# The order of instructions of a four-layer graph kernel, searched again with a store that counts until it lands

## The chip, the cores and the metric

The kernel runs on one core of one Trainium2 chip. The metric is the device time of one execution in microseconds (us), the median over several runs. A separate execution is recorded by the hardware profiler; its span can differ from the timed runs by a few microseconds. The engines are PE (matmul), DVE (vector), ACT (activation), POOL (GpSimd) and SP (SyncE, which here only issues transfers). PEld is PE's loading of weights, which runs beside its matmuls.

## The reference, cut to what matters

128 graphs of 64 nodes with 256 features go through four layers. Each layer is followed by a residual addition and a layer norm.

```python
# layer 0: gated graph network, five rounds l
m = h @ weight[l];  agg = A^T @ m           # A = (adj != 0)
h = gru_cell(agg, h)                        # r, z, n gates; tanh and sigmoid
x = layernorm(x + h * mask)
# layer 1: graph network with a wide hidden layer
h = (epsilon * x + adj @ x) @ W1 + b1       # 256 -> 1024
x = layernorm(x + silu(rmsnorm(h) * rms_weight) @ W2 + b2)
# layer 2: hyperbolic layer
x = layernorm(x + project(expmap0(adj @ logmap0(x))))
# layer 3: attention over neighbours
h = x @ W_w.T + W_b;  u = adj * exp(e_i + f_j + a_b)
x = layernorm(x + (u / sum(u)) @ h)
```

## The kernel before

Two graphs stand side by side on the 128 partitions, with a block-diagonal adjacency; four such blocks, eight graphs, form a group. There are 16 groups, and each passes through all four layers on its own. One extra stream ahead of them prepares weights. All is in 32-bit floats. The large products of layer 0 and of the first half of layer 1 use seven products of half blocks instead of eight (`gate`, `prod` and the sums in `sums`, lines 733 to 761), which costs DVE additions.

Memory is held in three sets of slots (`NF = 3`): group g uses set g % 3. A tile's tag says which slot it takes, and most tags have one buffer. Tag A holds, in one group, the tile `tA` of each round of layer 0 (L736, the differences of the state's halves), then the outputs of norms, and at the very end `o`, the result of the last `layer_norm`, from which the store to `out` is issued (L1116). Three groups later the same slot takes `tA` again, so the first subtraction of that group waits until the store has read the slot.

No instruction is placed by hand. `group(g)` records operations with a price in us for each engine that could do them, and with the buffers they read and write. `Flow.issue` then replays a planner, `Plan.advance`, which picks from up to four open groups (`WINDOW`) the operation that could start first by the plan's clocks, prices, waits for other operations (`HOPS` between engines), free PSUM banks (eight) and outstanding transfers. Ties and priorities are given by a rank: 0 prefers the oldest group, 1 the youngest (loads apart), and 2 and up the groups' remaining path minus a lag from `LAGS` per group. The string `CHOICES` has one digit for each stretch of planned time (`STRETCH`) and says which rank holds in it. The string was found by a search outside the kernel; the kernel only replays it. The resulting order is forced on each engine. Semaphores are placed by the framework from the data dependencies.

A transfer's operation has a size `kb`. Then the plan adds to its end a start cost, the transfer over a common bus and a landing cost, `DMA = (2.0, 330.0, 1.0)`, and whatever depends on it is ready only then:

```python
if o.kb:
    self.bus = max(self.bus, end + flow.DMA[0]) + o.kb / flow.DMA[1]
    end = self.bus + flow.DMA[2]
```

The final store carries no `kb`, so in the plan its slot is free 0.1 us after it starts. Some operations are marked `port`: those of POOL and a number of DVE operations with two inputs in SBUF. The plan lets no two of these overlap. The comparisons of adjacency blocks (L706), their rewriting (L896) and the small operations of the norms (L678, L1018 to L1041) carry no such mark.

The norms of all but the last two groups take the mean from sums gathered earlier, squares on ACT (L665), a power on POOL (L676) and a scaling on ACT or DVE (`scaled`, L334 and L335); the last two groups use DVE's statistics instead (L672).

Of the kernel before, what the change touches and what calls it, by code (L numbers as in the profile page):

```python
# [13 lines left out]
AF = mybir.ActivationFunctionType  # L14
OP = mybir.AluOpType
# [11 lines left out]
class Buf:  # L27


    def __init__(self, make, slot=None, bank=False):  # L30
        self.make, self.slot, self.bank = make, slot, bank
        self.ap, self.uses, self.left, self.after = None, [], 0, ()
# [21 lines left out]
class Plan:  # L54


    def __init__(self, flow):
        self.flow = flow
        ops = [o for s in flow.streams for o in s]
        self.need = [o.need for o in ops]  # L60
        self.at = [0.0] * len(ops)
        self.uses = {}
        self.clock = dict.fromkeys(flow.AHEAD, 0.75)
        self.queues = [{e: deque(o for o in s if e in o.ways) for e in self.clock} for s in flow.streams]
        self.banks = [0.0] * BANKS
        self.left, self.first, self.bus = len(ops), 0, 0.0
        self.lands = [0.0] * flow.TRANSFERS
        self.order, self.table, self.port = [], None, 0.0
# [60 lines left out]
class Flow:  # L129
# [11 lines left out]
    AHEAD = {"PE": 32, "DVE": 10, "ACT": 10, "POOL": 4, "SP": 2}  # L141


    HOPS = {"from PE": 0.25, "to PE": 0.3, "else": 0.1, "own": 0.0}

    SOONER = 0.4

# [2 lines left out]
    TRANSFERS = 8  # L150

    TABLE = 1.28
    WINDOW, STRETCH, LAGS = 4, 7.0, (0.0, 60.0, 150.0)
    CHOICES = ("0120330330303130310011121010201001100010002001222000010013000330100101111033330000333001101130100330"
               "0000031033000310101000311310101010000013101101101100010000013103010010101000100330110330000113003003"
               "1300130130100000010113001030300100100110333311103310110001000111110011110100111010130010011313010301"
               "110003301001110311310110011010200100000")

    BEHIND = mybir.DependencyInfo(mybir.DependencyClass.NoSync, mybir.DependencyReason.DATA)

# [44 lines left out]
    def hop(self, e, to):  # L205
        if e == to:
            return 0.0 if e == "PE" else self.HOPS["own"]
        return self.HOPS["from PE" if e == "PE" else "to PE" if to == "PE" else "else"]

# [11 lines left out]
    def issue(self):  # L221
        self.ways()
        ranks = (lambda s, o: (s, o.n), lambda s, o: (s if o.kb else -s, o.n), *(lambda s, o, lag=lag: (lag * s - o.way, s, o.n) for lag in self.LAGS))
        plan, until = Plan(self), 0.0
        for c in self.CHOICES:
            until += self.STRETCH
# [12 lines left out]
def kernel(  # L239
# [31 lines left out]
    nc = tc.nc  # L271
# [19 lines left out]
    flow = Flow(tc)  # L291
# [6 lines left out]
    def bank(name):  # L298
        return Buf(lambda: psum.tile([P, 512], F32, tag="bank", name=name), bank=True)
# [11 lines left out]
        return nc.tensor.matmul(o, lhsT, rhs, start=(k == 0), stop=(k == nk - 1))  # L311

    def pe(n, run, w, r):
        flow.op("PE", {512: 0.86, 256: 0.435, 128: 0.23, 1: 0.21}.get(n, 0.3), run, w, r)

    def turn(run, w, r):
        flow.op("PE", 0.11, run, w, r)
# [1 line left out]
    def dve(n, run, w, r, port=False):  # L319
        flow.op("DVE", 0.145 + 0.00105 * n, run, w, r, port=port)  # L320
# [3 lines left out]
    def act(n, run, w, r, sets=None):  # L324
        flow.op("ACT", 0.22 + 0.00077 * n, run, w, r, sets=sets)
# [5 lines left out]

    def scaled(n, o, i, scale, bias, w, r, port=()):

        flow.either([("ACT", 0.22 + 0.00077 * n, lambda: nc.scalar.activation(o(), i(), AF.Identity, bias=bias(), scale=scale())),  # L334
                     ("DVE", 0.145 + 0.00105 * n, lambda: nc.vector.tensor_scalar(o(), i(), scale(), bias(), OP.mult, OP.add))], w, r, port=port)  # L335

    def pool(us, run, w, r=()):
        flow.op("POOL", us, run, w, r, port=True)
# [5 lines left out]
    out_rows = out.rearrange("(g b t) n d -> g (t n) b d", b=NB, t=2)  # L344
# [45 lines left out]
    pow2 = const.tile([P, 2, NB], F32, name="pow2")  # L390
# [121 lines left out]
    for l in range(L):  # L512
        ps = bank("ps_wmT")
# [8 lines left out]
        for k in range(KD):  # L522
            for i, n in ((0, 2 * D), (1, D)):
                ps = bank("ps_wmih")
# [71 lines left out]
    def group(g):  # L596
        s = g % NF

        def tiny(name, shape=(P, NB), dt=F32):
            t = f"{name}{s}"  # L600
            return Buf(lambda: small.tile(list(shape), dt, tag=t, name=f"{name}_{g}"), slot=(t, 2))
# [54 lines left out]
        def layer_norm(y, st, tag, name, norm=None):  # L656

            mv = tiny("mv", (P, NB, 2))
            ve, rstd, off = tiny("ve", (P, 2, NB)), tiny("rstd", (P, 2, NB)), tiny("off")
            o = rows(tag, f"x_{name}")  # L660
            m = 2 if norm else 1
            if summed:
                dve(4, lambda: nc.vector.tensor_scalar(mv[:, :, 0], st[:, :, 0], -1.0 / D, None, OP.mult), [mv], [st])
                for b in range(NB):
                    act(500, lambda b=b: nc.scalar.activation(  # L665
                        o[:, b, :], y[:, b, :], AF.Square, bias=mv[:, b, 0:1], accum_out=st[:, b, 1:2]),
                        [(o, b), (st, (1, b))], [(y, b), mv])
                dve(8, lambda: nc.vector.scalar_tensor_tensor(  # L668
                    ve[:, :m, :], over(st[:, :, 1], m), 1.0 / D, eps2[:, :m, :], OP.mult, OP.add), [ve], [st])
            else:  # L670
                for b in range(NB):
                    dve(256, lambda b=b: nc.vector.bn_stats(st[:, b, :], y[:, b, :]), [(st, b)], [(y, b)])  # L672
                    dve(4, lambda b=b: nc.vector.bn_aggr(mv[:, b, :], st[:, b, :]), [(mv, b)], [(st, b)])
                dve(8, lambda: nc.vector.tensor_tensor(
                    ve[:, :m, :], over(mv[:, :, 1], m), eps2[:, :m, :], OP.add), [ve], [mv])
            pool(1.1, lambda: nc.gpsimd.tensor_tensor(rstd[:, :m, :], ve[:, :m, :], pow2[:, :m, :], OP.pow), [rstd], [ve])  # L676
            if norm:
                dve(4, lambda: nc.vector.scalar_tensor_tensor(  # L678
                    norm.tile(), rstd[:, 1, :], float(np.sqrt(D)), rstd[:, 0, :], OP.mult, OP.mult), [norm], [rstd])
            dve(4, lambda: nc.vector.scalar_tensor_tensor(  # L680
                off.tile(), mv[:, :, 0], 1.0 if summed else -1.0, rstd[:, 0, :], OP.mult, OP.mult), [off], [mv, rstd])
            for b in range(NB):
                scaled(256, lambda b=b: o[:, b, :], lambda b=b: y[:, b, :], lambda b=b: rstd[:, 0, b:b + 1],
                       lambda b=b: off[:, b:b + 1], [(o, b)], [(y, b), off, rstd], ("DVE",))
            return o
# [3 lines left out]
        if g == NG - 2:  # L689


            for k in range(KD):
                w = unit("h", (NG - 3) % NF, f"w1_{k}", (P, H), 2)
# [4 lines left out]
        ps = bank("ps_adjT")  # L698
# [189 lines left out]
        for n in range(2):  # L888
            ps = rows_of(hT, n)
            for j in range(2):  # L890
                b = 2 * n + j
# [93 lines left out]
        ps = bank("ps_ss")  # L985
# [16 lines left out]
        for h in range(NB // 2):  # L1002
            ps = bank("ps_o1")
            for j in range(2):
                b = 2 * h + j
# [6 lines left out]
        xn = tiny("n")  # L1012
        x2 = layer_norm(y1, st1, "A", "n1", xn)


        rn, fac, n2, ser = (tiny(t) for t in ("rn", "fac", "n2", "ser"))
        near = tiny("near", dt=I32)
# [11 lines left out]
        def series():  # L1029
# [5 lines left out]
                  for q in (11, 9, 7, 5, 3)),  # L1035
                v.tensor_add(ser.tile(), ser.tile(), one4),
                v.scalar_tensor_tensor(near.tile(), xn.tile(), SERIES_BELOW, one4, OP.is_lt, OP.mult)]
        dve(1150, series, [n2, ser, near], [xn])
        dve(4, lambda: nc.vector.scalar_tensor_tensor(fac.tile(), fac.tile(), 0.5, rn.tile(), OP.mult, OP.mult),
            [fac], [fac, rn])  # L1040
        dve(4, lambda: nc.vector.copy_predicated(fac.tile(), near.tile(), ser.tile()), [fac], [fac, near, ser])  # L1041
        tan = rows("B", "tan")
        for b in range(NB):
            flow.either([
                ("DVE", 0.3, lambda b=b: nc.vector.tensor_scalar(tan[:, b, :], x2[:, b, :], fac[:, b:b + 1], None, OP.mult)),
                ("ACT", 0.37, lambda b=b: nc.scalar.activation(tan[:, b, :], x2[:, b, :], AF.Identity, scale=fac[:, b:b + 1]))],
                [(tan, b)], [(x2, b), fac])
        us = tiny("ss")
        y2 = rows("y", "y2")
# [1 line left out]
        for h in range(NB // 2):  # L1051
            for j in range(2):
                b = 2 * h + j
                pe(256, lambda b=b, j=j, ps=sup[h]: matmul(
                    ps[:, j * D:(j + 1) * D], adjT[:, b, :], tan[:, b, :], 0, 1), [sup[h]], [adjT, (tan, b)])
            for j in range(2):
                b = 2 * h + j
# [32 lines left out]
        for b in range(NB):  # L1090
            ps = bank("ps_a")
            for k in range(KD):
                pe(256, lambda ps=ps, b=b, k=k: matmul(
                    ps[:, :D + 2], x3T[:, k, b * P:(b + 1) * P], wattT[:, k, :], k, KD), [ps], [(x3T, b // 2), wattT])
            act(4, lambda ps=ps, b=b: nc.scalar.activation(
                hw[:, b, D:], ps[:, D:D + 2], AF.Exp, bias=cs.tile()), [(hw, b)], [ps, cs], EXP)
            flow.either([
                ("ACT", 0.37, lambda ps=ps, b=b: nc.scalar.activation(
                    hw[:, b, :D], ps[:, :D], AF.Identity, scale=hw[:, b, D:D + 1])),
                ("DVE", 0.37, lambda ps=ps, b=b: nc.vector.tensor_scalar(  # L1100
                    hw[:, b, :D], ps[:, :D], hw[:, b, D:D + 1], None, OP.mult))], [(hw, b)], [ps, (hw, b)])
# [6 lines left out]
        for b in range(NB):  # L1108
            ps = bank("ps_att")
# [3 lines left out]
            dve(4, lambda b=b: nc.vector.tensor_mul(rd[:, b:b + 1], rd[:, b:b + 1], hw[:, b, D + 1:]), [(rd, b)], [(rd, b), (hw, b)])  # L1113
            onto_rows(y3, b, st3, ps, 0, lambda b=b: rd[:, b:b + 1], x3, [(rd, b)])
        o = layer_norm(y3, st3, "A", "n3")
        flow.op("SP", 0.1, lambda: nc.sync.dma_start(out_rows[g], o.tile()), (), [o])  # L1116

    for g in range(NG):
        flow.stream()
# [34 lines left out]
```

## Time and profile before

| | |
|---|---|
| time, median of 3 runs | 2393.74 us (2393.57 to 2394.22) |
| span in the profile | 2397.7 us |
| PE busy | 2338.0 us, 98% |
| PE's weight loads busy | 2045.3 us, 85% |
| DVE, ACT, POOL busy | 1878.5, 1248.8, 343.4 us |
| last PE instruction ends before the span's end | 11.8 us |
| output stores | 16 of 512 KB, median 2.9 us from issue to landing |

A matmul record's end is modelled, so the sum of single durations means little here; the idle time of PE and the share of the clock that it was granted say how far the span is from PE's own work. Numbers in the timeline count from the first instruction. A line number is that of the kernel; many products share the lines of helpers, so tiles tell them apart.

### The profile page before, as it was taken

The numbers are of one execution on the slowest core, as the hardware profiler recorded it, in microseconds if no ns is written. First come the engines' busy times: TensorE is split into PE (matmuls) and PEld (weight loads), VectorE is DVE, ScalarE is ACT, GpSimd is POOL, SyncE is SP. The second block draws the span as 40 slices with busy tenths as digits, with TensorE's granted clock in tenths as the row PEclk, the third lists the DMA queues.
The fourth block names the chain that finished last, engine by engine and source line by source line (L and its number), as shares of the span: only waits on it lengthen the run. The fifth ranks groups of instructions, "written<-read, shape, count | busy, mean of one in ns | idle before, by whom it ended". The sixth has DMA issues, their size and how long they took to land.

```text
span 2397.7 us, 32662 instructions
## 1 busy us (share of the span) xinstructions
PE 2338.0 (98%) x11938; PEld 2045.3 (85%) x11938; DVE 1878.5 (78%) x4291; ACT 1248.8 (52%) x2671; POOL 343.4 (14%) x272
## 2 busy tenths in 40 slices
PE   9999998999999999999999999999999999999986
PEld 8888887888888888888888888888888888888854
DVE  6778978778878878778778788868877886887866
ACT  3333455666455555465555555554454467445364
POOL 1300111411010201112120110210111131011011
PEclk9999999999999999999999999999999999999998
DMA  3000001000000000000000000000000000000000
GB/s 122 10 1 1 12 1 38 1 21 1 29 1 27 3 1 30 1 27 3 1 29 1 29 1 27 3 7 23 1 10 21 10 1 21 27 1 10 27 9 18
DMA packets 39728, 36.22 MB, mean 15 GB/s; under 512 B 9956, under 2 KB 38656, under 8 KB 39568
## 3 DMA queue, kind: packets, MB, share of 16 engines
q1 hardware_dynamic: 37840, 32.25, 4.3%
q8 instruction: 95, 1.56, 0.3%
q10 hardware_dynamic: 1328, 1.31, 0.2%
q0 software_dynamic: 400, 0.57, 0.1%
q14 instruction: 65, 0.53, 0.1%
HBM read 25.74 MB, written 8.39 MB: 14 GB/s over the span
## 4 chain that ended last, share of the span: by engine, by line
PE 91%; DVE 5%; ACT 2%; DMA 1%; issue 1%; POOL 0%; ACTq 0%; POOLq 0%; DVEq 0%
PE p_v L753 11%; PE p_w L753 11%; PE p_r L753 11%; PE ps_o L311 9%; PE ps_agg L311 7%; PE p_hy L759 6%; PE p_u L753 6%; PE p_iy L759 6%; PE p_ix L759 4%; PE p_hx L759 4%; PE ps_hr L627 3%; PE ps_a L311 2%; PE p_vh L940 2%; PE p_1h L940 2%; PE p_wh L940 2%; PE ps_wmih L311 1%
## 5 line engine op out<-in xcount | busy, mean ns | idle before, releaser
L676 POOL TENSOR_TENSOR rstd<-ve,pow 128x4 f32<-128x4 f32 (+1 forms) x64 | 79.5, 1242 | 1296.9 <-DVE ve L668 1186.5
L311 PE MATMUL ps_o<-w2s,hid 128*128 128x256 f32 x1024 | 234.2, 381 | 0.3 <-ACT hid L1000 0.3
L311 PEld LDWEIGHTS ps_o<-w2s,hid 128*128 128x128 f32 x1024 | 194.3, 191 | 26.5 <-ACT hid L1000 0.3
L753 PE MATMUL p_v<-tA,w_h 128*128 128x256 f32 x640 | 172.7, 380 | 0.8 <-DVE V L804 0.8
L753 PE MATMUL p_v<-tB,w_a 128*128 128x256 f32 x640 | 171.4, 379 | 0.0
L753 PE MATMUL p_r<-hT,w_h 128*128 128x256 f32 x640 | 171.1, 382 | 0.2 <-ACT U L329 0.2
L753 PE MATMUL p_r<-agg,w_a 128*128 128x256 f32 x640 | 167.1, 381 | 0.2 <-ACT agg L329 0.2
L807 ACT ACTIVATE U<-U,half_b 128x512 f32<-128x512 f32 (+1 forms) x160 | 93.9, 628 | 133.6 <-DVE U L804 133.4
L311 PEld LDWEIGHTS ps_agg<-edge,hr 128*128 128x128 f32 x1024 | 138.3, 191 | 7.9 <-ACT hr L329 0.2
L329 ACT COPY agg<-ps_agg 128x512 f32<-128x512 f32 x148 | 86.1, 583 | 109.6 <-PE ps_agg L311 108.4
L311 PE MATMUL ps_agg<-edge,hr 128*128 128x128 f32 x1024 | 140.3, 275 | 0.0
L759 PE MATMUL p_hy<-tA,w_hn 128*128 128x256 f32 x480 | 131.9, 381 | 6.9 <-DVE tA L736 4.7
L329 ACT COPY hr<-ps_hr 128x512 f32<-128x512 f32 x120 | 70.1, 584 | 129.2 <-PE ps_hr L627 128.5
L779 DVE SCALAR_TENSOR_TENSOR hnb<-p_hy,half_b,hs 128x256 f32<-128x256 f32 x240 | 108.6, 479 | 35.3 <-PE p_hy L759 34.0
L753 PEld LDWEIGHTS p_r<-agg,w_a 128*128 128x128 f32 x640 | 120.4, 191 | 16.5 <-ACT agg L329 0.9
L759 PE MATMUL p_iy<-tB,w_in 128*128 128x256 f32 x480 | 132.3, 383 | 2.2 <-DVE V L824 2.2
L753 PEld LDWEIGHTS p_v<-tA,w_h 128*128 128x128 f32 x640 | 119.2, 191 | 16.7 <-DVE V L804 1.2
L753 PEld LDWEIGHTS p_v<-tB,w_a 128*128 128x128 f32 x640 | 119.7, 190 | 16.0 <-issue 0.5
L807 ACT ACTIVATE V<-V,half_b 128x256 f32<-128x256 f32 (+1 forms) x160 | 87.2, 585 | 80.5 <-DVE V L804 80.2
L753 PEld LDWEIGHTS p_r<-hT,w_h 128*128 128x128 f32 x640 | 116.0, 191 | 13.8 <-ACT U L329 0.4
L1000 ACT ACTIVATE hid<-hid,cols 128x512 f32<-128x512 f32 x128 | 85.5, 717 | 62.9 <-DVE hid L998 62.8
L334 ACT ACTIVATE x_n<-y,off,rstd 128x256 f32<-128x256 f32 x173 | 90.8, 589 | 45.4 <-DVE off L680 45.4
(262 smaller groups left out, 5819.4 us busy)
## 6 DMA issues: line engine op xcount, KB each, us to landing
x<-in_x_dram SPq DMA_DIRECT2D x16, 512.0 KB, 3.6
xr<-in_x_dram SPq DMA_DIRECT2D x16, 512.0 KB, 3.4
out_dram<-x_n SPq DMA_DIRECT2D x16, 512.0 KB, 2.9
edge<-in_adj_dram SPq DMA_DIRECT2D x32, 64.0 KB, 2.3
wm<-in_L_gnn_weight_dram SPq DMA_DIRECT2D x5, 256.0 KB, 5.1
w2s<-in_L_gnn_W_dram SPq DMA_DIRECT2D x1, 1024.0 KB, 9.0
w<-in_L_gnn_W_dram SPq DMA_DIRECT2D x2, 512.0 KB, 3.4
w_in_L_gnn_w_hh_dram<-in_L_gnn_w_hh_dram ACTq DMA_DIRECT2D x1, 512.0 KB, 5.4
```

What stands on the lines that cost most here:

```text
L311: return nc.tensor.matmul(o, lhsT, rhs, start=(k == 0), stop=(k == nk - 1))
L329: flow.either([("ACT", 0.22 + 0.00077 * n, lambda: nc.scalar.copy(o(), i())), ("DVE", 0.145 + 0.00105 * n, lambda: nc.vector.tensor_copy(o ...
L334: flow.either([("ACT", 0.22 + 0.00077 * n, lambda: nc.scalar.activation(o(), i(), AF.Identity, bias=bias(), scale=scale())), ("DVE", 0.145 ...
L627: turn(lambda j=j, c=c: nc.tensor.transpose(ps[:, j * D + c * P:j * D + (c + 1) * P], src[:, c, (2 * n + j) * P:(2 * n + j + 1) * P], iden ...
L676: pool(1.1, lambda: nc.gpsimd.tensor_tensor(rstd[:, :m, :], ve[:, :m, :], pow2[:, :m, :], OP.pow), [rstd], [ve])
L753: pe(256, lambda i=i, w=w, c=c: nc.tensor.matmul(ps[:, c * HR:(c + 1) * HR], w[:, m, c * P:(c + 1) * P], v[i][0](), start=first and i == 1 ...
L759: pe(256, lambda: nc.tensor.matmul(ps[:, j * HR:(j + 1) * HR], w[:, m, :], v[0](), start=first, stop=True, skip_group_check=True), [ps], [ ...
L779: dve(300, lambda: nc.vector.scalar_tensor_tensor(out(n, c)(), ps[:, j * HR:(j + 1) * HR], b(c), x(), OP.add, OP.add), [(hnb, (n, c))], [p ...
L807: act(256 if len(w) == 1 else 512, lambda: nc.scalar.activation(o(), src(), AF.Tanh, bias=half_b[:, i * KD + c:i * KD + c + 1], scale=0.5) ...
L940: pe(256, lambda c=c: nc.tensor.matmul(ps[:, c * HR:(c + 1) * HR], w1f[:, w, (2 * q + c) * P:(2 * q + c + 1) * P], v[0](), start=first and ...
L1000: act(512, lambda v=v, c=c: nc.scalar.activation(v, v, AF.Silu, scale=rmsc(c)), parts, [*parts, cols], SILU)
```

## The change

The program's operations stay as they are. The planner's constants are set anew, and `CHOICES` is replaced by what a new search with these constants kept: of many orders, the one that was steadiest when durations are disturbed. The old string has 339 digits for stretches of 7 us, the new one 588 for stretches of 4 us. The old ranks were 0, 1, and lags of 0, 60 and 150 as 2, 3 and 4; the new ones are 0, 1, and lags of 60 and 150 as 2 and 3, so a 3 of the old string and a 2 of the new one mean the same. The purpose is that the plan agrees better with what the chip does: above all, the slot of the stored result is free only when the store has landed.

```diff
-        self.clock = dict.fromkeys(flow.AHEAD, 0.75)
+        self.clock = dict.fromkeys(flow.AHEAD, 2.5)
...
-    HOPS = {"from PE": 0.25, "to PE": 0.3, "else": 0.1, "own": 0.0}
+    HOPS = {"from PE": 0.22, "to PE": 0.15, "else": 0.06, "own": 0.0}
...
-    WINDOW, STRETCH, LAGS = 4, 7.0, (0.0, 60.0, 150.0)
-    CHOICES = ("0120330330303130310011121010201001100010002001222000010013000330100101111033330000333001101130100330"
+    WINDOW, STRETCH, LAGS = 4, 4.0, (60.0, 150.0)
+    CHOICES = ("0001210202220220200202001001011000011111001011100001101010000011101000001000101020011100002211002111"
...
-        flow.op("PE", {512: 0.86, 256: 0.435, 128: 0.23, 1: 0.21}.get(n, 0.3), run, w, r)
+        flow.op("PE", {512: 0.863, 256: 0.433, 128: 0.219, 1: 0.2}.get(n, 0.3), run, w, r)
...
     def scaled(n, o, i, scale, bias, w, r, port=()):
-        flow.either([("ACT", 0.22 + 0.00077 * n, ...
+        flow.either([("ACT", 0.3 + 0.0008 * n, ...
...
     # layer_norm
-                    act(500, lambda b=b: nc.scalar.activation(
+                    act(400, lambda b=b: nc.scalar.activation(
                         o[:, b, :], y[:, b, :], AF.Square, bias=mv[:, b, 0:1], accum_out=st[:, b, 1:2]),
...
-            pool(1.1, lambda: nc.gpsimd.tensor_tensor(rstd ... pow
+            pool(1.25, lambda: nc.gpsimd.tensor_tensor(rstd ... pow
...
-        dve(1150, series, [n2, ser, near], [xn])
+        dve(1400, series, [n2, ser, near], [xn])
...
-                ("ACT", 0.37, lambda b=b: nc.scalar.activation(tan ...
+                ("ACT", 0.43, lambda b=b: nc.scalar.activation(tan ...
...
-                ("ACT", 0.37, lambda ps=ps, b=b: nc.scalar.activation(hw ...
+                ("ACT", 0.47, lambda ps=ps, b=b: nc.scalar.activation(hw ...
...
-        flow.op("SP", 0.1, lambda: nc.sync.dma_start(out_rows[g], o.tile()), (), [o])
+        flow.op("SP", 0.5, lambda: nc.sync.dma_start(out_rows[g], o.tile()), (), [o], kb=512)
```

`act(n)` prices an operation at 0.22 + 0.00077 n us and `dve(n)` at 0.145 + 0.00105 n us, so 500 to 400 and 1150 to 1400 are changes of 0.605 to 0.528 and 1.35 to 1.615 us.

More of the change, by code (lines that the diff above doesn't have):

```diff
@@ L152 @@
     TABLE = 1.28
-    WINDOW, STRETCH, LAGS = 4, 7.0, (0.0, 60.0, 150.0)
-    CHOICES = ("0120330330303130310011121010201001100010002001222000010013000330100101111033330000333001101130100330"
-               "0000031033000310101000311310101010000013101101101100010000013103010010101000100330110330000113003003"
-               "1300130130100000010113001030300100100110333311103310110001000111110011110100111010130010011313010301"
-               "110003301001110311310110011010200100000")
+    WINDOW, STRETCH, LAGS = 4, 4.0, (60.0, 150.0)
+    CHOICES = ("0001210202220220200202001001011000011111001011100001101010000011101000001000101020011100002211002111"
+               "0010002212011101012212212100222012102200120001000200200012010111210112220000000202201121220010001010"
+               "0101010111011100020120010000001100000000010010010020012002000010100022210001100000200000220210100100"
+               "0011110100100021120110001101100200002101000000100001000011010111011010100010010010200102001101000100"
+               "2011010001000100000011000010101102000012100000100020221100000001000010001100000000100102112000002011"
+               "0021000010011011100111000000100100110100022111011111110001100101110110110000111000011000")
     BEHIND = mybir.DependencyInfo(mybir.DependencyClass.NoSync, mybir.DependencyReason.DATA)
@@ L332, in scaled @@
     def scaled(n, o, i, scale, bias, w, r, port=()):
-        flow.either([("ACT", 0.22 + 0.00077 * n, lambda: nc.scalar.activation(o(), i(), AF.Identity, bias=bias(), scale=scale())),
+        flow.either([("ACT", 0.3 + 0.0008 * n, lambda: nc.scalar.activation(o(), i(), AF.Identity, bias=bias(), scale=scale())),
                      ("DVE", 0.145 + 0.00105 * n, lambda: nc.vector.tensor_scalar(o(), i(), scale(), bias(), OP.mult, OP.add))], w, r, port=port)
@@ L675, in layer_norm @@
                     ve[:, :m, :], over(mv[:, :, 1], m), eps2[:, :m, :], OP.add), [ve], [mv])
-            pool(1.1, lambda: nc.gpsimd.tensor_tensor(rstd[:, :m, :], ve[:, :m, :], pow2[:, :m, :], OP.pow), [rstd], [ve])
+            pool(1.25, lambda: nc.gpsimd.tensor_tensor(rstd[:, :m, :], ve[:, :m, :], pow2[:, :m, :], OP.pow), [rstd], [ve])
             if norm:
@@ L1045, in group @@
                 ("DVE", 0.3, lambda b=b: nc.vector.tensor_scalar(tan[:, b, :], x2[:, b, :], fac[:, b:b + 1], None, OP.mult)),
-                ("ACT", 0.37, lambda b=b: nc.scalar.activation(tan[:, b, :], x2[:, b, :], AF.Identity, scale=fac[:, b:b + 1]))],
+                ("ACT", 0.43, lambda b=b: nc.scalar.activation(tan[:, b, :], x2[:, b, :], AF.Identity, scale=fac[:, b:b + 1]))],
                 [(tan, b)], [(x2, b), fac])
@@ L1097, in group @@
             flow.either([
-                ("ACT", 0.37, lambda ps=ps, b=b: nc.scalar.activation(
+                ("ACT", 0.47, lambda ps=ps, b=b: nc.scalar.activation(
                     hw[:, b, :D], ps[:, :D], AF.Identity, scale=hw[:, b, D:D + 1])),
```

## The prediction

> **What bounds the kernel now.** I read the page first, then the busy time by stage, then what the matmul engine (PE) waited for, then the tile of the output store, and last the timeline around the longest waits. The page:
>
> ```profile
> PE 2338.0 (98%) x11938; PEld 2045.3 (85%) x11938; DVE 1878.5 (78%) x4291; ACT 1248.8 (52%) x2671; POOL 343.4 (14%) x272
> PEclk9999999999999999999999999999999999999998
> ```
>
> PE is the bound almost everywhere. The change adds and removes no matmul, so all it can win is PE's idle time and the time PE runs at a reduced clock. The windows view measures both; its columns are window, length, busy us (and count) of PE, PEld, DVE, ACT, POOL, then granted clock, DMA share, GB/s:
>
> ```profile
> 0.00:60.00 60.00, 57.13 (x297) 48.09 (x298) 37.09 (x94) 20.57 (x45) 6.80 (x16) 1.00 0.39 122
> 60.00:2280.00 2220.00, 2191.98 (x11303) 1934.48 (x11301) 1766.80 (x3968) 1161.46 (x2496) 317.33 (x242) 1.00 0.04 12
> 2280.00:2320.00 40.00, 36.81 (x120) 20.05 (x120) 29.61 (x54) 26.35 (x44) 8.14 (x5) 0.96 0.04 14
> 2320.00:2355.00 35.00, 32.80 (x148) 28.30 (x148) 16.74 (x57) 18.02 (x32) 2.64 (x2) 0.95 0.00 1
> 2355.00:2398.00 43.00, 19.28 (x72) 14.35 (x72) 28.27 (x122) 22.37 (x56) 8.49 (x7) 0.73 0.07 25
> ```
>
> Idle PE: 2.9 us in the head, 28.0 in the middle, 5.4 in the two windows before the end, 23.7 in the last 43 us. The granted clock falls to one half for short pieces after idle time: two of 3.4 us and one of 6.8 us in the middle, where half of 13.6 us, 6.8 us, is lost. So the middle loses 28.0 + 6.8 = 34.8 us. From 2280 to 2355 it is 5.4 + 0.04 x 40 + 0.05 x 35 = 8.8 us.
>
> Who ends PE's idle time, in the waits view (us in total, times, longest):
>
> ```profile
> PE ps_sup L311 <- DVE tan L1045: 5.9, 1, 5.9
> PE ps_T L617 <- ACT x_n L334: 5.8, 1, 5.8
> PE p_hy L759 <- DVE hnb L779: 5.7, 3, 3.6
> PE p_hy L759 <- DVE tA L736: 4.7, 3, 2.6
> ```
>
> The first two lie in the last 43 us. The other two are in the middle, and behind them stands the store. The view of the output tensor shows who waits for it and how long a store takes from issue to landing:
>
> ```profile
>   DVE tA L736: 19.3, 6
> DMA to landing us min/median/max: 2.8/2.9/4.6
> ```
>
> Tile tA takes tag A, which has one buffer for each of the three group slots; the last norm's output of an earlier group sits there until its store has read it. The timeline of the worst case (start, us, what, idle before):
>
> ```profile
> 1808.98 0.38 SPq L1116 DMA_DIRECT2D out_dram<-x_n  x1
> 1813.67 0.69 DVE L736 TENSOR_TENSOR tA<-hT 128x512 f32<-128x512 f32 x1 [5.61 <-DMA out_dram<-x_n]
> 1816.21 1.22 PE L759 MATMUL p_hy<-hT,w_hn 128*128 128x256 f32 x2 [3.63 <-DVE hnb L779]
> ```
>
> DVE runs in order: while it waits 5.61 us at tA, everything queued behind it (the L779 sums, L804, L824 additions that free PSUM banks) waits too, and PE runs dry 3.63 us later. Of the six waits, one (at 928 us, 1.2 us) costs PE nothing; the five others stand in these windows:
>
> ```profile
> 401.00:409.00 8.00, 5.48 (x36) 5.15 (x37) 5.78 (x13) 5.00 (x11) 1.21 (x2) 1.00 0.35 103
> 1344.00:1352.00 8.00, 6.47 (x35) 5.66 (x34) 5.76 (x18) 1.79 (x4) 0.00 (x0) 1.00 0.20 68
> 1631.00:1639.00 8.00, 5.84 (x20) 4.79 (x21) 7.30 (x12) 5.44 (x12) 0.00 (x0) 0.79 0.21 67
> 1813.00:1823.00 10.00, 6.79 (x19) 5.52 (x20) 7.17 (x19) 4.00 (x12) 1.01 (x1) 0.66 0.00 0
> 2051.00:2059.00 8.00, 6.11 (x30) 5.08 (x30) 6.73 (x13) 2.98 (x6) 0.00 (x0) 1.00 0.25 83
> ```
>
> Idle 2.5 + 1.5 + 2.2 + 3.2 + 1.9 = 11.3 us, and lost to the clock 0.21 x 8 + 0.34 x 10 = 5.1 us: 16.4 us of the middle's 34.8 come from the store.
>
> A second family has nothing to do with it: DVE held up while a long POOL instruction runs.
>
> ```profile
> 1932.44 2.35 POOL L906 TENSOR_TENSOR xb<-x_n,b_r 128x1024 f32<-128x1024 f32 x1
> 1932.51 2.30 DVE L678 SCALAR_TENSOR_TENSOR n<-rstd 128x4 f32<-128x4 f32 x1 [1.75 <-POOL rstd L676]
> 1937.88 2.50 PE L940 MATMUL p_1h<-aggm,w1f 128*128 128x256 f32 x5 [2.25 <-ACT aggm L329]
> ```
>
> A 128x4 operation that elsewhere takes 0.16 us takes 2.30 beside the POOL addition. PE stalls behind such cases at 299 (0.76), 413 (1.77), 473 and 479 (0.85, 1.15), 805 (1.31) and 1938 us (2.25, and 1.7 at half clock): 9.8 us. The remaining 34.8 - 16.4 - 9.8 = 8.6 us are small waits spread over the middle.
>
> [...] this trace's 512 KB stores from SyncE took 2.8 to 4.6 us, so the plan's old price of 0.1 us was wrong in kind. [...]
>
> **The change part by part.** (1) The store is priced 0.5 us of SyncE and 512 KB of transfer: by the plan's constants 2.0 + 512/330 + 1.0 = 4.6 us to landing, at the trace's worst (4.6) and above its median (2.9). The next user of slot A now becomes ready in the plan about when it is in fact ready, and other DVE work is put ahead of it. Of 16.4 us I take 15 back: some margin for stores that land late. Bounds: 16.4 if all is hidden, 8 if the search can hide only half. (2) Durations. A norm's ACT scaling goes from 0.417 to 0.505 (the trace has 2.08 us for four in a row, 0.52); the Square from 0.605 to 0.528 (four start 0.49 apart); the series from 1.35 to 1.615 (1.61 from 1935.94 to 1937.55); ACT's tan from 0.37 to 0.43 (498 ns) and hw from 0.37 to 0.47 (474 ns); POOL's pow from 1.1 to 1.25 (mean 1242 ns); a 256-wide product from 0.435 to 0.433 (26 instructions of ps_o in 5.61 us, two to a product: 0.432). All of them move closer to the trace. These act on the 8.6 us of small waits; I take half, 4 us, with bounds 0 and 8. (3) Not touched: which DVE operations clash with POOL. L706, L896 and the small norm operations carry no port mark before or after. The new order meets such clashes by chance as the old one did: 9.8 us before, 9.8 after, change 0, with bounds +8 and -6. (4) The end. From 2280 to 2355, 4.4 us of PE idle and the half clock after it wait for a norm's ACT operations, which the old prices made too short; two groups of work are still there to fill it. I take 3 of 8.8 us, bounds 0 and 7. The last 43 us are one chain of norm, support, norm, attention and store through DVE, ACT and POOL; an order can't shorten a chain, so 0, bounds +4 and -5. (5) The start clock of 2.5, finer stretches of 4 us, dropping lag 0 and the shorter hops add no instruction and no semaphore; I price them at 0: PE covers 57.1 of the first 60 us, and the hops are hidden wherever PE has queued work. Choosing ACT or DVE anew can shift load, but DVE is at 78% and ACT at 52%, with PE above both.
>
> Sum: 15 + 4 + 0 + 3 + 0 = 22 us. 2393.7 - 22 = 2371.7; I say 2372.
>
> **The rivals.** (A) The store's wait goes, but the new order brings its own stalls of about half that size, since every place in the order is shuffled and POOL clashes and the clock's penalty are still unknown to the plan: gain 5 to 13, about 2384. For it: the 9.8 us of the untouched family. Against: steadiness is what the kept order was chosen for. (B) Nearly everything in the middle goes: 30 of 34.8 and 7 of 8.8 us: about 2356. For it: PE has work for other groups at each of these places. Against: part (3). (C) Slower: shorter hops (to PE 0.3 to 0.15, from PE 0.25 to 0.22) let the plan put producers closer to their users; stalls that were slack become real, and two or three long ones with half clock cost 5 to 7 us each, as at 1813: +16 against a store gain of about 6, about 2404. For it: the plan's slack against reality shrinks. Against: fixed prices now agree better with the trace. (D) No change: the store's wait becomes another wait of DVE at the same buffer, about 2394.
>
> **How the numbers follow.** Forecast (2360 to 2380) 0.50; A (2380 to 2389) 0.19; B (below 2360) 0.13; D 0.05; C 0.13. Faster by over 0.2% is forecast, A and B: 0.82; same 0.05; slower 0.13. The range goes from 2355, leaving half of B out, to 2396, leaving most of C out.
>
> **What would show it.** Right: the output's view shows no DVE wait at tA, or under 3 us in all; the middle loses 12 to 20 us instead of 34.8, and fewer half-clock pieces stand there; PE's busy time stays near 2338, with equal counts on PE and equal instruction lengths; the last 43 us still hold some 24 us of PE idle. Wrong: the store's wait stays above 10 us; or it is gone and PE's waits in the middle still add up to 25 us or more under other names; or the end grows by over 5 us.

## The result, and the profile after

| | before | after |
|---|---|---|
| time, median of 4 runs each on one chip | 2393.98 us (2393.57 to 2398.42) | 2379.72 us (2378.54 to 2380.74) |
| ratio | | 0.9936, 95% 0.9919 to 0.9953 |
| span in the profile | 2397.7 us | 2376.8 us |

The kernel is 14.3 us faster, 22 were forecast. A later comparison with more runs (9 of before, 5 of after) gives a ratio of 0.9930, 0.9916 to 0.9943; the medians lie 17.7 us apart there. The two differ because before scatters: 21 runs of it in experiment 1 lie between 2393.6 and 2399.5 us, while the five of after in experiment 5 lie between 2379.1 and 2380.1. The fastest executions of the two kernels are 15.0 us apart in the first comparison and 14.4 in the second.

The page of after, its busy times and its row of the granted clock:

```profile
PE 2329.7 (98%) x11938; PEld 2039.0 (86%) x11938; DVE 1892.0 (80%) x4293; ACT 1247.2 (52%) x2667; POOL 341.2 (14%) x272
PEclk9999999999999999999999999999999999999997
```

The number of matmuls is the same. PE's busy time is 8.3 us less, most of which is no work saved: before's span has 43.5 us at half clock and after's 30.3, and half of the difference is 6.6 us. The same five stages as before, in the windows view of after (window, length, busy us and count of PE, PEld, DVE, ACT, POOL, then granted clock, DMA share, GB/s):

```profile
0.00:60.00 60.00, 57.45 (x285) 48.05 (x286) 35.09 (x92) 19.59 (x41) 4.21 (x12) 1.00 0.38 122
60.00:2256.00 2196.00, 2185.43 (x11312) 1929.63 (x11311) 1779.19 (x3962) 1160.99 (x2496) 316.85 (x246) 1.00 0.04 12
2256.00:2299.00 43.00, 37.39 (x133) 20.09 (x132) 30.48 (x60) 29.73 (x48) 8.15 (x5) 1.00 0.04 13
2299.00:2334.00 35.00, 31.61 (x141) 27.26 (x141) 20.15 (x70) 16.55 (x33) 5.25 (x4) 0.94 0.00 1
2334.00:2377.00 43.00, 17.85 (x72) 14.00 (x72) 27.11 (x114) 20.32 (x51) 6.74 (x5) 0.70 0.07 25
```

PE idles 2196.00 - 2185.43 = 10.6 us in the middle (28.0 before), and no half-clock piece is left there (13.6 us at half clock before). But the two windows before the last, 78 us here and 75 before, hold 5.6 + 3.4 us of idle time against 5.4, and the last 43 us hold 25.2 us of idle at a clock of 0.70 against 23.7 at 0.73. Who ends PE's waits in after (us in total, times, longest):

```profile
PE ps_T L619 <- ACT x_n L336: 10.0, 1, 10.0
PE ps_sup L313 <- ACT tan L1048: 5.9, 1, 5.9
PE p_ix L761 <- DVE V L826: 3.3, 2, 2.6
...
PE p_hx L761 <- DVE tA L740: 1.7, 1, 1.7
```

The first two stand in the last 43 us; ps_T was 5.8 before. The output's view in after, which named tA with 19.3 us before:

```profile
L1118 SPq DMA_DIRECT2D out_dram<-x_n x16: 383/388/395, 392.6 to 2373.0; - x16
its engine sat idle before it (us, times) until:
who waited for it (us, times):
busy tenths in 40 slices 0000000000000000000000000000000000000000
DMA to landing us min/median/max: 2.8/2.9/3.3
```

The list of those who waited is empty. In the median the stores take as long as before, and nobody waits for them.

### The profile page after: what moved, and what is told of

It reads as the page before. It is cut to its first block, busy times and chain, and to the rows that moved or that the text cites. A ratio compares the mean times of both kernels' runs of the same rounds, so it can differ in the third digit from the quotient of the medians.

```text
span 2376.8 us, 32667 instructions
## 1 busy us (share of the span) xinstructions
PE 2329.7 (98%) x11938; PEld 2039.0 (86%) x11938; DVE 1892.0 (80%) x4293; ACT 1247.2 (52%) x2667; POOL 341.2 (14%) x272
## 4 chain that ended last, share of the span: by engine, by line
PE 93%; DVE 5%; ACT 1%; issue 1%; POOL 0%; POOLq 0%; ACTq 0%; DVEq 0%
PE p_v L755 11%; PE p_r L755 11%; PE p_w L755 11%; PE ps_o L313 9%; PE ps_agg L313 7%; PE p_hy L761 6%; PE p_u L755 6%; PE p_iy L761 6%; PE p_hx L761 4%; PE p_ix L761 4%; PE ps_hr L629 3%; PE ps_a L313 2%; PE p_vh L942 2%; PE p_wh L942 2%; PE p_1h L942 2%; PE ps_sup L313 1%
## 5 line engine op out<-in xcount | busy, mean ns | idle before, releaser
L755 PEld LDWEIGHTS p_r<-agg,w_a 128*128 128x128 f32 x640 | 120.0, 190 | 16.4 <-issue 1.0
L755 PEld LDWEIGHTS p_r<-hT,w_h 128*128 128x128 f32 x640 | 114.6, 190 | 13.9 <-ACT V L331 0.4
L667 ACT ACTIVATE x_n<-y,mv 128x256 f32<-128x256 f32 x168 | 83.3, 498 | 58.8 <-DVE mv L665 58.7
L336 ACT ACTIVATE x_n<-y,off,rstd 128x256 f32<-128x256 f32 x160 | 84.0, 589 | 42.6 <-DVE off L682 42.6
```

Source lines behind the costliest of these rows:

```text
L336: flow.either([("ACT", 0.3 + 0.0008 * n, lambda: nc.scalar.activation(o(), i(), AF.Identity, bias=bias(), scale=scale())), ("DVE", 0.145 + ...
L667: act(400, lambda b=b: nc.scalar.activation(o[:, b, :], y[:, b, :], AF.Square, bias=mv[:, b, 0:1], accum_out=st[:, b, 1:2]), [(o, b), (st, ...
L755: pe(256, lambda i=i, w=w, c=c: nc.tensor.matmul(ps[:, c * HR:(c + 1) * HR], w[:, m, c * P:(c + 1) * P], v[i][0](), start=first and i == 1 ...
```

## The experiments

To compare stages I split a span at the first ps_hid matmul, the beginning of the last groups' output work: "middle" is the time up to it, "end" the time from it. In before these are 2286.4 and 111.2 us, in after 2262.8 and 114.0. Where idle time or half clock "in the middle" is given without other bounds, it is counted as in the windows above, from 60 us to some 6 us before that matmul, so the stall and the half-clock piece that stand there in most executions are largely left out. Each profile is one execution, and one half-clock piece of 3.4 us more or less moves it by 1.7 us.

**1. The kernel before once more.** No edit.

> The kernel before, unchanged, to see how its executions spread and whether the granted clock moves with the time. Theory: the 5 us by which the profiled execution (span 2397.7) lies above the median of 2393.98 are half-clock pieces that come in some executions only; then executions near 2398 show a lower mean granted clock (about 0.991) than executions near 2393 (about 0.993), and a profile near 2393 loses under 7 us to the clock in its middle. Rival: the times spread with no change of clock.

Measured: 2396.58 us, 21 runs from 2393.63 to 2399.54. This profile has a span of 2392.5 us, 5.2 below the one that the prediction was read from, and 3.4 us at half clock in the middle instead of 13.6. Half of the 10.2 us between them is 5.1 us, so the two executions differ by little but the number of PE stalls beside which a half-clock piece stands. The other runs agree in kind: those of a mean granted clock of 0.993 take 2395.1 us in the mean, those of 0.991 take 2399.0. The store's wait is the same in both (DVE's waits in this run):

```profile
DVE tA L736 <- DMA out_dram<-x_n: 19.0, 6, 5.3
```

So the baseline for the shares below is this profile: middle 2281.0, end 111.5 us.

**2. Before, without the wait for the store.**

```diff
-        flow.op("SP", 0.1, lambda: nc.sync.dma_start(out_rows[g], o.tile()), (), [o])
+        flow.op("SP", 0.1, lambda: nc.sync.dma_start(out_rows[g], w2s[:, :NB, :]), (), [o])
```

> The kernel before in the same order; each output store takes its 512 KB from a constant tile, so nothing waits for slot A to be read. It leaves out the storing of the results: the output is not the network's. Theory (the store's landing costs what the profile shows): no DVE wait at tA for a store, and 11 to 16 us less than before, 2378 to 2383. Rival (PE would have stalled a little later anyway, on whatever DVE had next): under 5 us less, 2389 or more.

Measured: 2378.74 us, ratio 0.9920 (0.9904 to 0.9936), 18.0 us less, where 11 to 16 were expected. The edit leaves the plan's order as it was. The output's view of this run:

```profile
L1116 SPq DMA_DIRECT2D out_dram<-w2s x16: 427/500/620, 389.7 to 2267.9; - x16
its engine sat idle before it (us, times) until:
who waited for it (us, times):
busy tenths in 40 slices 0000000000000000000000000000000000000000
DMA to landing us min/median/max: 4.9/5.0/6.5
```

Nobody waits, although these stores take 5.0 us: it was the wait and not the traffic that cost. The middle shrinks from 2281.0 to 2266.7, by 14.3 us; the other 3.6 us come at the end (111.5 to 107.9), because the last store no longer waits for the last norm (it is issued at 2267.9), which is this edit's own gift and not the change's.

**3 and 4. Before with short POOL additions, with and without the store's wait.** The additions on POOL keep their place in the order and add 4 columns only:

```diff
-    ... nc.gpsimd.tensor_tensor(o(), x0(), x1(), OP.add)
+    ... nc.gpsimd.tensor_tensor(*((t[:, :4] if n == 512 else t[:, :, :4]) for t in (o(), x0(), x1())), OP.add)
...
-        xb = rows("y", "xb")
-    ... nc.gpsimd.tensor_tensor(xb.tile(), x1.tile(), over(b2_r.tile(), NB), OP.add)
+        xb = Buf(lambda: y0.tile(), slot=(f"y{s}", 1))
+    ... nc.gpsimd.tensor_tensor(xb[:, :, :4], x1[:, :, :4], over(b2_r[:, :4], NB), OP.add)
```

> The kernel before in the same order; the three long POOL additions (squares of the hidden layer, x + b2, x + W_b) touch only 4 columns of each row, and the second works in place on the tile that holds its slot. It leaves out most of these additions. Theory (PE stalls behind DVE operations that wait for a long POOL addition, 9.8 us in the profile before): 7 to 12 us less than before, 2382 to 2387, and the stalls at 299, 413, 473, 805 and 1938 us gone while the store's five stay. Rival (those stalls have other causes, DVE is merely full there): under 3 us less.

> Both edits on the kernel before, in the same order: stores from a constant tile, and POOL additions of 4 columns (it leaves out the storing of the results and most of these additions). Theory (two separate causes): the gains add up within 4 us, 18 to 28 us less than before, 2366 to 2376, with a middle that loses under 10 us. Rival (one hides behind the other): no more than the larger of the two gains alone plus 3 us.

Measured: 2383.26 us (ratio 0.9941, 0.9927 to 0.9956), 13.5 less; and with the store's edit 2363.66 (0.9859, 0.9844 to 0.9875), 33.1 less, beyond the 18 to 28 expected. 18.0 + 13.5 = 31.5: the two causes add up, as the prediction took them. In experiment 3 the PE stalls at 299, 413, 473, 479 and 805 us are gone, the one at 1938 is down to 0.1, and the store's stalls stay (402, 1339, 1625, 1806 and 2038 us). The POOL family is dearer than expected: 13.5 against 7 to 12.

**5 and 6. After once more, and after with short POOL additions** (the edit of 3).

> The changed kernel, unchanged, beside many runs of the kernel before. Theory (it has no half-clock piece in its middle): it spreads less than the kernel before, within 4 us, and lies 15 to 19 us below it: 2377 to 2382. Rival (its few runs so far were lucky): it spreads as widely as before, some 10 us.

> The changed kernel in the same order; the three long POOL additions touch only 4 columns of each row, and the second works in place on the tile that holds its slot. It leaves out most of these additions. Theory (what is left in the middle of the changed kernel, 10.6 us of PE idle, are DVE operations that wait for a long POOL addition): 7 to 11 us less than the changed kernel, 2368 to 2373, with under 3 us of PE idle left in the middle. Rival (the new order's stalls are its own, for want of DVE time): under 3 us less.

Measured: 2379.53 us (0.9930, 0.9916 to 0.9943), with 1.0 us from the lowest to the highest of five runs, and 2363.84 (0.9864, 0.9851 to 0.9878), 15.7 less than after. PE's idle in the middle falls from 10.5 to 0.5 us, so of what the records show as idle after the change, nearly all is this family. One of its cases in the timeline of after (start, us, what, idle before):

```profile
738.95 2.69 POOL L343 TENSOR_TENSOR x_n<-x_n,wb_r 128x1024 f32<-128x1024 f32 x1 [5.32 <-PE ps_T L619]
739.45 2.73 DVE L878 SCALAR_TENSOR_TENSOR hT<-V,hT 128x512 f32<-128x512 f32 x1
744.75 1.14 PE L313 MATMUL ps_a<-wattT,x3T 128*128 128x258 f32 x4 [0.92 <-DVE U L806]
```

The same DVE operation took 0.69 us at 737.39. Here it takes 2.73 us, 2 us more, beside the POOL addition of 2.69 us; what is queued behind it on DVE comes late, and PE waits 0.92 us for one of these five microseconds later.

It was expected to give 7 to 11 us and gave 15.7, more than the 10.0 us of idle that went. The idle time before an instruction counts only what is beyond the modelled end of the one ahead, and in the trace of after the record of a 256-wide matmul lasts 379 ns while the next matmul starts 216 ns after its start (medians): by these two numbers, an estimate, about 0.16 us of every stall does not show. Counted from start to start, by sums of my own from the trace that no view gives and that depend by some us on what is taken as the usual distance, the excess in the middle is 39.2 us in experiment 1, 25.3 in 2, 11.7 in 4, 23.0 in after and 7.5 here: 23.0 - 7.5 = 15.5, about the gain.

A rival is that something waited for the results of these additions, which the edit makes earlier too. The waits view names for that only ACT (14.4 us in all in experiment 5) and one weight load (0.4 us), and no DVE operation. Experiment 9, which does all of the additions, tells more.

**7 and 8. The store's price alone.** Before with the new price and the old string of choices; after with the old price and the new string (both filled up with zeros, since the plan takes more stretches):

```diff
-        for c in self.CHOICES:
+        for c in self.CHOICES + "0" * 40:
...
-        flow.op("SP", 0.1, ... (), [o])
+        flow.op("SP", 0.5, ... (), [o], kb=512)
```

> The kernel before with one part of the change alone: the store has its 0.5 us and 512 KB in the plan; durations, hops, ranks and the old string stay (40 digits 0 are added at its end), so the order is a new one that nobody searched. Theory (counting the store is what removes its wait): DVE waits at tA for a store under 3 us in all, against 19 before. The time is open, since an unsearched order brings stalls of its own: 2385 to 2420. Rival (the wait went because another order happened to avoid it): 10 us or more of such waits stay.

> The changed kernel with one part undone: the store is 0.1 us and lands at once in the plan; the new durations, hops and string stay (40 digits 0 are added at its end), so this too is an unsearched order. Theory (counting the store is what removes its wait): DVE waits at tA for a store come back, 8 us or more in all; time 2385 to 2420. Rival (the new durations alone keep tA away from the store): they stay under 3 us.

Measured: 2600.28 us (1.0850, 1.0835 to 1.0865) and 2559.53 (1.0682, 1.0668 to 1.0697), both far outside of what either theory expected. With another price every later choice meets another situation, and in neither case did the string fit any more. In 7, PE waits 54.8 us at a place where before waits 1.4 (PE's waits):

```profile
PE ps_hr L627 <- DVE hT L878: 54.8, 23, 4.7
```

In 7 no DVE operation waits for a store. In 8 some do again (the output's view):

```profile
  DVE tA L738: 5.4, 3
```

That is the direction expected, at a size between the two theories. These runs do not say what the price alone is worth: with either string it cost far more than it won. What a new search with the old prices would have won, no run shows.

**9. After with POOL's additions in pieces of 256 columns.** Squares in two pieces, others in four, all the work done:

```diff
-    ... nc.gpsimd.tensor_tensor(o(), x0(), x1(), OP.add)
+    ... [nc.gpsimd.tensor_tensor(*((t[:, i * 256:(i + 1) * 256] if n == 512 else t[:, i, :]) for t in (o(), x0(), x1())), OP.add) for i in range(2 if n == 512 else NB)]
...
-    ... nc.gpsimd.tensor_tensor(xb.tile(), x1.tile(), over(b2_r.tile(), NB), OP.add)
+    ... [nc.gpsimd.tensor_tensor(xb[:, b, :], x1[:, b, :], b2_r.tile(), OP.add) for b in range(NB)]
```

> The changed kernel in the same order and with the same arithmetic; each long POOL addition is cut into pieces of 256 columns (two for the squares, four for x + b2 and x + W_b). Theory (a DVE operation that finds POOL inside an addition waits for the rest of that one instruction): no such wait is longer than one piece, about 0.8 us instead of up to 2.4, and 5 to 11 of the 15.7 us that these additions cost come back: 2369 to 2375. Rival (POOL's next piece is taken first, so DVE waits for all of them, and four pieces take 3.1 us instead of 2.4): the same time within 3 us, or slower.

Measured: 2371.55 us, ratio 0.9898 (0.9881 to 0.9915), 8.0 less than experiment 5. (Experiments 9 to 12 ran on other chips than 5; the fastest execution of before was 2393.5 to 2394.2 us on all of them.) DVE is now held up more often (77 operations by over 0.15 us, 57 in after) but never by more than 0.6 us, and in sum for 30.0 instead of 47.9 us; PE's idle in the middle is 3.9 us. ACT's waits for POOL's sums rise from 14.4 to 18.0 us at the same time, so it was the hold on DVE, and not the results' lateness, that cost these 8 us.

**10. After with the first tanh moved ahead.** The end had grown, and the timeline of after shows where. Group 14's norm n is ready at 2335.93; its tanh (L1066) comes at 2342.27:

```profile
2335.78 0.15 DVE L1065 SCALAR_TENSOR_TENSOR n<-n 128x4 f32<-128x4 f32 x1
2335.96 1.30 ACT L1048 ACTIVATE tan<-x_n,fac 128x256 f32<-128x256 f32 x3 [0.76 <-DVE n L1065]
...
2338.63 0.38 ACT L1060 ACTIVATE y<-ps_sup 128x256 f32<-128x256 f32 x1 [1.37 <-PE ps_sup L313]
...
2340.98 1.28 ACT L1066 ACT_TABLE_LOAD   x1
...
2342.27 0.30 ACT L1066 ACTIVATE th<-n 128x4 f32<-128x4 f32 x2
```

The plan puts the load of the table, and group 14's tanh with it, behind group 15's four squares (L1060), which wait for PE. In before the load came ahead of the squares, with group 14's tanh right after it:

```profile
2361.24 1.28 ACT L1064 ACT_TABLE_LOAD   x1
2362.53 0.20 ACT L1064 ACTIVATE th<-n 128x4 f32<-128x4 f32 x1
2363.69 0.38 ACT L1058 ACTIVATE y<-ps_sup 128x256 f32<-128x256 f32 x1 [0.95 <-PE ps_sup L311]
...
2368.05 0.20 ACT L1064 ACTIVATE th<-n 128x4 f32<-128x4 f32 x1 [2.67 <-DVE n L1063]
```

One load serves both groups' tanh in before too; what differs is its place. The edit moves group 14's tanh to the place behind the last tan, and group 15's back to where it is needed (a function that rearranges the finished order, no work added):

```diff
-        for eng, o in plan.order:
+        for eng, o in earlier(plan.order, self.ends):
...
+    late = [order.pop(place(o)) for o in (n15, urn15, th15)]
+    order[place(prior) + 1:place(prior) + 1] = late
+    one = order.pop(place(th14))
+    order.insert(max(place(u) for u in (*tan15, n14)) + 1, one)
```

> The changed kernel; near the end, ACT's tanh of the last group but one, with its table load, stands ahead of the last group's four squares instead of behind them, and on DVE the two small operations that wait for those squares stand behind the last group but one's own chain. PE's order is untouched. Theory (the end grew by 3 us because the plan put both tanh behind one table load, which holds the earlier group for the later one): PE's wait of 9.95 us at ps_T falls to 5 to 7 us and the time by 2 to 5 us: 2375 to 2378. Rival (the last group's chain ends the span, and it gets later by what the other wins): within 1 us of the changed kernel.

Measured: 2376.50 us, ratio 0.9919 (0.9905 to 0.9934), 3.0 less than experiment 5. The end falls from 114.6 to 111.2 us, before's value. There is still one load for both tanh, now ahead of the squares, so the sharing that the expectation blames is not the cause; the place is. Its timeline, and PE's wait:

```profile
2338.04 1.28 ACT L1066 ACT_TABLE_LOAD   x1
2339.33 0.20 ACT L1066 ACTIVATE th<-n 128x4 f32<-128x4 f32 x1
2339.44 0.37 ACT L1060 ACTIVATE y<-ps_sup 128x256 f32<-128x256 f32 x1
```

```profile
PE ps_T L619 <- ACT x_n L336: 6.5, 1, 6.5
```

**11 and 12. Both edits together, with pieces of 256 and of 128 columns.** The edits of 9 and 10; in 12 squares go in four pieces and others in eight.

> The changed kernel with both edits: POOL additions in pieces of 256 columns, and the earlier tanh in the end. Theory (two separate places): the gains add up within 2 us, 7 to 16 us under the changed kernel: 2364 to 2373. Rival: no better than the better of the two alone.

> The changed kernel with the earlier tanh, and with the POOL additions in pieces of 128 columns (four for the squares, eight for the others). Theory (a wait is as long as one piece): pieces of about 0.5 us instead of 0.8 win another 2 to 4 us over the pieces of 256: 2365 to 2367. Rival (POOL's own work grows from some 243 to some 320 us, and each piece is one more chance to hold DVE up): no better than 2369, or worse.

Measured: with 256 columns 2368.98 us (2368.81 to 2369.22), ratio 0.9887 (0.9872 to 0.9902). That is 10.5 us below after (8.0 + 3.0 = 11.0: they add up) and 25.1 below before, the fastest kernel of the study that does all the work. With 128 columns 2384.81, ratio 0.9957 (0.9943 to 0.9971), 15.8 more than with 256 and slower than after itself (0.9930 in experiment 5). The timeline of 12 shows the largest part of why:

```profile
446.84 1.70 POOL L343 TENSOR_TENSOR sqt<-sqt,sqh 128x128 f32<-128x128 f32 x4
...
447.17 8.50 DVE L880 SCALAR_TENSOR_TENSOR hT<-hT,V 128x512 f32<-128x512 f32 x1
...
453.43 1.69 POOL L343 TENSOR_TENSOR sqt<-sqt,sqh 128x128 f32<-128x128 f32 x4
455.70 0.69 DVE L738 TENSOR_TENSOR tA<-hT 128x512 f32<-128x512 f32 x1
...
457.00 1.19 PE L761 MATMUL p_hx<-tA,w_hn 128*128 128x256 f32 x2 [5.18 <-DVE tA L740]
```

and the same operations in 11:

```profile
446.51 0.73 DVE L880 SCALAR_TENSOR_TENSOR hT<-hT,V 128x512 f32<-128x512 f32 x1
...
446.64 2.33 POOL L343 TENSOR_TENSOR sqt<-sqt 128x256 f32<-128x256 f32 x2
...
447.27 1.10 DVE L738 TENSOR_TENSOR tA<-hT 128x512 f32<-128x512 f32 x1
```

In 12 one DVE operation lasts 8.50 us, beside five sums of four pieces each that POOL runs back to back, and PE then waits 5.18 us for what is queued behind it; 6.8 us at half clock follow, which cost half of that. These 8.6 us are over half of the 15.5 by which the two middles differ (2271.5 and 2256.0); where the others went was not traced. Without this one operation DVE is held up for less than in 11, 15.6 us in sum instead of 30.0, so elsewhere the shorter pieces hold it up less, as the theory said. In 11 POOL's two pieces take 2.33 us beside the two DVE operations of 0.73 and 1.10 us, and 1.40 us at 452.04, where no DVE operation is slowed.

## Why the prediction came out as it did

The chain of experiments 1, 2, 4, 6 and 5 splits the change of the span between 1 and 5 (2392.5 to 2378.3, 14.2 us less). The shares add up by construction, and each is uncertain by a half-clock piece or so (1.7 us):

| step | predicted | measured | from |
|---|---|---|---|
| the store is counted | -15 | -14.3 | middle, experiments 1 and 2: 2281.0 to 2266.7 |
| POOL beside DVE | 0 | +1.9 | cost in before 13.3 (2 to 4: 2266.7 to 2253.4), in after 15.2 (5 to 6: 2263.8 to 2248.6) |
| durations, and all else of the new order in the middle | -4 | -4.8 | 4 to 6: 2253.4 to 2248.6 |
| the end | -3 | +3.1 | 1 to 5: 111.5 to 114.6 |
| sum (unrounded) | -22 | -14.2 | |

1. The store. Right in mechanism and in size: no wait at tA is left, and taking the wait away from the unchanged order is worth 14.3 us in the middle. That the price keeps it away, and not a new order that happened to avoid it, rests on experiments 7 and 8 alone: no such wait with the price in a second order, 5.4 us without it, which is less than the theory's 8. The size has some luck in it. The 16.4 us that it was read from hold 5.1 us of half clock, and experiment 1 has one piece at a store's stall (at 404 us), 1.7 us. Up to the first ps_hid matmul PE's idle time falls by 11.0 us from experiment 1 to 2 (28.7 to 17.7); with these 1.7 us that makes 12.7, and the rest of the 14.3 is the part of each stall that the idle column does not show. Two errors of opposite sign met in that term.

2. Nearer durations. The middle does gain 4.8 us beyond the store and the POOL family. But durations, hops, the start clock, the string's finer stretches and the choice of the steadiest all stand behind that number, and no run tells them apart; experiments 7 and 8 show why one of them alone cannot be tried with a string that was found for the others. That the durations did it was argued and is not shown.

3. POOL beside DVE. The prediction said that the new order does nothing about it, since no price tells the plan how much longer a DVE operation takes beside a POOL addition (2.73 us instead of 0.69 in the case under experiments 5 and 6); that is so. The cost itself was put at 9.8 us and is 13.3: 10.1 us of idle time goes from experiment 2 to 4 (17.7 to 7.6 up to the first ps_hid matmul), and some 3 us more are not in the idle column. The change of +1.9 lies within the bounds given (+8, -6) and hardly beyond what one half-clock piece makes.

4. The end. This is the term that was mis-sized, and it makes 6 of the 8 us between forecast and result: 3 us were expected back from the stretch before the last 43 us, and the last 43 us were put at 0 because an order can't shorten a chain. But an order can lengthen one: the load of the table and group 14's tanh now stand behind group 15's squares, and the tanh comes 6.3 us after its input (2.6 in experiment 10), on the path that sets the end. Experiment 10 moves it and the end is 111.2 us, so this costs 3.4 of the 6 us. The 3 us forecast for the stretch before did not come either: even then the end is only 0.3 us under before's. Why that stretch won nothing stays open.

The measured 2379.7 us lie 0.3 us inside the forecast's band, which ends at 2380 where rival A's begins, and before alone scatters by more; the time cannot choose between the two, the stages can. Rival A (new stalls of the new order's own, 2384 us) was right as far as the end goes, and wrong for the middle, which loses 10.6 us, less even than the 12 to 20 that the prediction named as its sign. Rival B (below 2360) would have needed the POOL family gone too: experiment 6, where it is, has 2363.84.

## What to carry to other kernels

A planner that counts a transfer as done when it is issued puts the next user of its source too early, and what is queued behind that user on its engine comes late too (19.0 us of DVE's waits at tA, 14.3 us of the span here); price the slot until the landing, and search again, for a string of choices can lose all its worth under other prices (8.5% and 6.8% slower here). After such a search look at the end of the program by itself, since a better order in the middle can lose a few microseconds where one chain sets the time (3.1 us here). And where POOL's additions hold DVE up, try them in pieces: 256 columns won 8.0 us here against 512 and 1024, while 128 lost 15.8 us against 256, for the most part at one place of one order.

## What the runs showed of the hardware beyond what was expected

- Beside POOL additions in pieces of 128 columns (0.42 us each, back to back) one DVE operation lasted 8.50 us, some twenty pieces long; beside pieces of 256 (0.7 to 0.8 us) no DVE operation lost over 0.6 us, and POOL's two-piece sums took up to 2.3 us beside DVE operations where others took 1.4. The 8.50 us were measured in this one case, and what makes the difference between the two lengths was not isolated.
- Runs of the kernel before on one chip lie up to 10 us apart (2393.7 to 2403.2), and half-clock pieces that come in some executions and not in others are a large part of it: of the 5.2 us between two profiled executions they are 5.1. In every profile the pieces start a whole number of 3.413 us apart, so I divide the profiles into stretches of that length. The stall of 2.18 us that ends at 1633 us of before lies within one stretch, and the next runs at half clock. In experiment 1 the same stall is divided between two stretches, and the clock stays full (windows views of before, then of experiment 1, PE's busy time first and the clock third from the end):

```profile
1630.53:1633.94 3.41, 1.23 (x6) 0.75 (x6) 2.64 (x5) 3.37 (x8) 0.00 (x0) 1.00 0.00 0
1633.94:1637.35 3.41, 3.41 (x10) 2.66 (x9) 3.38 (x7) 1.33 (x2) 0.00 (x0) 0.50 0.49 150
```

```profile
1628.99:1632.41 3.42, 2.70 (x16) 1.88 (x14) 2.75 (x6) 2.38 (x5) 0.00 (x0) 1.00 0.00 0
1632.41:1635.82 3.41, 1.96 (x9) 1.75 (x10) 3.31 (x6) 2.20 (x5) 0.00 (x0) 1.00 0.00 0
1635.82:1639.23 3.41, 3.41 (x20) 3.00 (x19) 3.34 (x6) 2.98 (x6) 0.00 (x0) 1.00 0.55 156
```

  Counted over all 14 profiles, a stretch at full clock was followed by one at half clock 99 times. In 91 of these PE idled for more than 1.98 us of the 3.41, in the other 8 for 1.42 to 1.91; the profiles of before and after hold 12 of the 91, with 2.03 to 3.30 us. Only two stretches with more idle time than 1.98 us were followed by full clock, both in the first half microsecond of a profile. So this stall cost 1.7 us, half of the stretch, in the one profile and nothing in the other, and what differs is where it falls among the stretches. After repeated within 1.0 us in one set of runs and 2.2 us in the other.
- A store from a constant buffer took 5.0 us to land where the same 512 KB from the norm's output took 2.9, and this cost nothing, as nobody waited.
